# Compression sums of a two-layer kernel: from VectorE products to TensorE matmuls over rows fetched back from DRAM, with the statistics of chunks 8 to 15 held in place

## The chip, the cores and the metric

The kernel runs on one core of one Trainium2 chip, as one program. The metric is device time of that core in microseconds (us). The core has TensorE (PE in the profile, its weight loads PEld), VectorE (DVE), ScalarE (ACT), GpSimd (POOL) and SyncE (SP, which here only issues DMAs). All data is float32; a float32 matmul shows as two MATMUL records in the trace.

## What is computed

A batch of 4 sequences of 512 tokens with 512 features goes through two transformer layers. Layer 0 is a compressed sparse attention with 16 heads of 128 plus a local window, and a mixture of 8 experts; layer 1 is a plain attention with 16 heads of 32 and another mixture. The part that the change touches is the start of layer 0. Cut to what matters:

```python
xn = layernorm(x)                                   # 4 x 512 x 512
w_log = (xn @ Wcmp + bcmp).reshape(4, 128, 4)       # one logit a token, groups of 4 tokens
w_cmp = softmax(w_log, axis=-1)
entries = einsum('bcr,bcrh->bch', w_cmp, xn.reshape(4, 128, 4, 512))
ck = rope(rmsnorm(entries @ Wk + bk), block_ends)   # 128 compressed keys a sequence
cv = entries @ Wv + bv                              # and their values
# every head's queries score ck, keep the 8 best and mix cv; a local window attention is added
```

So each sequence's 512 normalized rows are reduced to 128 entries, each a weighted sum of four neighbouring rows.

## The kernel before

**Chunks and copies of the input.** The 2048 tokens are 16 chunks of 128 rows; chunks 0 to 3 are sequence 0, 4 to 7 sequence 1, and so on. `acc` holds the rows in SBUF. `layernorm(n, ...)` takes the statistics of chunk n on VectorE (`bn_stats` L221, its aggregate L223, an addition L224), the inverse root on GpSimd (L225, for chunks from 4 on also L227), makes the normalized rows `xn` (on VectorE for chunks 0 to 3, on ScalarE at L234 for the others), writes them to the DRAM tensor `xnd` (L237; chunks 4 to 7 from ScalarE's queue, the others from SyncE's) and turns them on TensorE (`trx`, L242) into `xnT`, the transposed copy that every product reads (copy at L243). Before the change `xnd` is read only much later, by the expert gathers.

**Steps.** The main loop runs over 32 steps (g, b): 8 groups of two heads, and in each the 4 sequences. Step i computes the attention of its group and sequence and projects the queries, keys and values of step i+1 in between, by seven half-size products (`first`, `second`, ..., `fifth`, all matmuls at L661, VectorE sums at L696 to L725). `project(0)` stands ahead of the loop. Inside a step the order is `scores` of head 0, `first`, `scores` of head 1, `second`, `context` of head 0, `third`, `context` of head 1, `fourth`, `fifth`, `output`.

**Work hung into the first steps.** `jobs0` hangs further work into places (i, t) of the steps: sequence 0 and 1 are normalized ahead of the loop, sequence 2's chunks 8 to 11 in step 0, sequence 3's chunks 12 to 15 in step 1. `compress(b, pool)` is a generator of four parts; those of sequence 0 run ahead of the loop, and those of b = 1, 2, 3 in steps 0, 1, 2. Part 1 transposes the compression logits (`wt`, L584), makes the softmax weights `w1` and builds `wd`, 128x512, by four VectorE multiplications of the identity (L596). Part 2 spreads `wd` over all partitions by a matmul with a matrix of ones (`wB`, L599) and, for each of four feature blocks, multiplies `xnT` by it (`prod`, L603) and adds groups of four (L604) into `entT`. Part 3 multiplies `entT` by Wk and Wv (`kv`, L609) and normalizes and rotates `ck`. Part 4 turns `ck` (`trck`, L619) into `ckT`, which the scores `sp` (L744) of the sequence's step read.

**What sets the order.** The tile framework's scheduler reorders the instructions of each engine by its own estimate of when their inputs are ready; every engine then runs its list strictly in order and waits by semaphores. `tc.keep_in_program_order(x)` pins x behind the instruction that was written just before it on the same engine. In `layernorm` only the statistics of chunks below 4 are pinned (`pin`). PSUM tiles come from three rings: `mm` (3 banks: products, output), `sc` (3: scores, contexts, `wB`, `kv`) and `tr` (2: transposes). SyncE's DMA list is in order too.

Of the kernel before, what the change touches and what calls it, by code (L numbers as in the profile page):

```python
# [12 lines left out]
F32 = mybir.dt.float32  # L13
I32 = mybir.dt.int32
AF = mybir.ActivationFunctionType
ALU = mybir.AluOpType
AX = mybir.AxisListType
# [3 lines left out]
P = 128  # L21
B, S, HID = 4, 512, 512
T = B * S
NT = T // P
TC = S // P
KC = HID // P
NH, D = 16, 128
RATIO = 4
C = S // RATIO
# [20 lines left out]
def two_layers(ctx: ExitStack, tc: tile.TileContext, a: dict, out: bass.AP, large: bass.AP):  # L50


    FEW = 32
    nc = tc.nc
    V, G, A, PE = nc.vector, nc.gpsimd, nc.scalar, nc.tensor
# [14 lines left out]
    sp0 = setup.enter_context(tc.tile_pool(name="setup", bufs=2, side="right"))  # L70


    def psum(tag, name):
        return ps.tile([P, 512], F32, tag=tag, name=name, bufs={"mm": 3, "sc": 3, "tr": 2}[tag])
# [53 lines left out]
    xnT = keep.tile([P, KC, T], F32, tag="xnT", name="xnT")  # L128
    x_v = a["x"].rearrange("(n p) h -> p n h", p=P)

    xnd = dram.tile([T, HID], F32, tag="xnd", name="xnd")
# [43 lines left out]

    ident = const.tile([P, P], F32, tag="ident", name="ident")
    make_identity(nc, ident)
    nhalf = const.tile([P, 8], F32, tag="nhalf", name="nhalf")
    G.memset(nhalf, -0.5)
    A.activation(small.tile([P, 8], F32, tag="warm", name="warm", bufs=1), nhalf, AF.Exp)  # L180
    ones_sq = const.tile([P, P], F32, tag="ones_sq", name="ones_sq")
    G.memset(ones_sq, 1.0)
# [32 lines left out]
    def layernorm(n, pool, bank, scaled=False):  # L215

        pin = tc.keep_in_program_order if n < TC else (lambda x: x)
        st = small.tile([P, 6], F32, tag="st", name=f"st_{n}")  # L220
        pin(V.bn_stats(st, acc[:, n, :]))  # L221
        mv = small.tile([P, 2], F32, tag="mv", name=f"mv_{n}")
        V.bn_aggr(mv, st)  # L223
        V.tensor_scalar(mv[:, 1:2], mv[:, 1:2], 1e-5, None, ALU.add)  # L224
        G.tensor_tensor(mv[:, 1:2], mv[:, 1:2], nhalf[:, 0:1], ALU.pow)  # L225
        if scaled:
            G.tensor_scalar(mv[:, 0:1], mv[:, 0:1], mv[:, 1:2], -1.0, ALU.mult, ALU.mult)  # L227
        made = {}

        def rows():  # L230
            tag = "ctx" if n in (2, 3) else "xn"
            xn = made["xn"] = (wk0 if n in (2, 3) else pool).tile([P, HID], F32, tag=tag, name=f"xn_{n}")
            if scaled:
                A.activation(xn, acc[:, n, :], AF.Identity, scale=mv[:, 1:2], bias=mv[:, 0:1])  # L234
            else:
                pin(V.tensor_scalar(xn, acc[:, n, :], mv[:, 0:1], mv[:, 1:2], ALU.subtract, ALU.mult))
            (nc.scalar if TC <= n < 2 * TC else nc.sync).dma_start(out=xnd[ts(n, P), :], in_=xn)  # L237

        def turn():
            xn, tr = made["xn"], bank("tr", f"trx_{n}")  # L240
            for k in range(KC):
                pin(PE.transpose(tr[:, ts(k, P)], xn[:, ts(k, P)], ident))  # L242
            A.copy(xnT[:, :, ts(n, P)], tr.rearrange("p (k t) -> p k t", k=KC))  # L243
        return rows, turn
# [302 lines left out]
    lv = const0.tile([P, TC, 3, D + 1], F32, tag="lv", name="lv")  # L547
# [11 lines left out]
    def squares(x, n, pool, name, extra=1.0):  # L559

        sq = pool.tile([P, D], F32, tag="sq", name=f"sq_{name}", bufs=1)
        ss = small.tile([P, n], F32, tag=f"ss{n}", name=f"ss_{name}", bufs=4)
        for h in range(n):
            A.activation(sq, x[:, h, :], AF.Square, accum_out=ss[:, h : h + 1])  # L564
        G.tensor_scalar(ss, ss, D * 1e-6, extra, ALU.add, ALU.mult)
        G.tensor_tensor(ss, ss, nhalf[:, 0:n], ALU.pow)  # L566
        return ss

    def rotate(x, tt1, tt2, n, pool, name):

        r1 = pool.tile([P, n, R], F32, tag="r1", name=f"r1_{name}", padded_shape=[P, 6, R] if n > 1 else None, bufs=1)
        r2 = pool.tile([P, n, R], F32, tag="r2", name=f"r2_{name}", padded_shape=[P, 6, R] if n > 1 else None, bufs=1)
        V.tensor_tensor(r1, x[:, :, 0:R], tt1, ALU.mult)
        V.tensor_tensor(r2[:, :, 0:32], x[:, :, 32:R], tt2[:, :, 0:32], ALU.mult)
        V.tensor_tensor(r2[:, :, 32:R], x[:, :, 0:32], tt2[:, :, 32:R], ALU.mult)
        V.tensor_tensor(x[:, :, 0:R], r1, r2, ALU.add)

    def compress(b, pool):

        w_row = row_w[b]  # L580

        wt = psum("tr", f"wt_{b}")
        for r in range(RATIO):
            PE.transpose(wt[:, ts(r, P)], w_row.rearrange("p (c r) -> p r c", r=RATIO)[:, r, :], ident)  # L584
        w1 = pool.tile([P, RATIO], F32, tag="w1", name=f"w1_{b}", bufs=1)
        V.tensor_reduce(w1, wt.rearrange("p (r k m) -> p r k m", k=KC, m=FEW)[:, :, :, 0], AX.X, ALU.add)
        V.tensor_scalar(w1, w1, bcmp[:, 0:1], None, ALU.add)
        mx = pool.tile([P, 1], F32, tag="wmx", name=f"wmx_{b}", bufs=1)
        V.tensor_reduce(mx, w1, AX.X, ALU.max, negate=True)
        sm = pool.tile([P, 1], F32, tag="wsm", name=f"wsm_{b}", bufs=1)  # L590
        A.activation(w1, w1, AF.Exp, bias=mx, accum_out=sm)
        V.reciprocal(sm, sm)
        V.tensor_scalar(w1, w1, sm, None, ALU.mult)
        wd = pool.tile([P, C, RATIO], F32, tag="prod", name=f"wd_{b}", bufs=1)
        for r in range(RATIO):
            V.tensor_scalar(wd[:, :, r], ident, w1[:, r : r + 1], None, ALU.mult)  # L596
        yield
        wB = psum("sc", f"wB_{b}")
        PE.matmul(wB, lhsT=ones_sq, rhs=wd.rearrange("p c r -> p (c r)"), start=True, stop=True)  # L599
        entT = pool.tile([P, KC, C], F32, tag="entT", name=f"entT_{b}", bufs=1)  # L600
        for k in range(KC):
            prod = pool.tile([P, C, RATIO], F32, tag="prod", name=f"prod_{b}_{k}", bufs=1)
            V.tensor_tensor(prod.rearrange("p c r -> p (c r)"), xnT[:, k, ts(b, S)], wB, ALU.mult)  # L603
            V.tensor_reduce(entT[:, k, :], prod, AX.X, ALU.add)  # L604
        yield
        kv = psum("sc", f"kv_{b}")
        for i, w in enumerate((wk, wv)):
            for k in range(KC):
                PE.matmul(kv[:, ts(i, D)], lhsT=entT[:, k, :], rhs=w[:, k, :],  # L609
                          start=(k == 0), stop=(k == KC - 1))  # L610
        V.tensor_tensor(cv[:, b, 0:D], kv[:, ts(1, D)], bkv[:, 1, :], ALU.add)
        ck = pool.tile([P, 1, D], F32, tag="ck", name=f"ck_{b}", bufs=1)
        V.tensor_tensor(ck[:, 0, :], kv[:, ts(0, D)], bkv[:, 0, :], ALU.add)
        ss = squares(ck, 1, pool, f"ck_{b}")
        rotate(ck, t1c, t2c, 1, pool, f"ck_{b}")
        A.activation(ck[:, 0, :], ck[:, 0, :], AF.Copy, scale=ss[:, 0:1])
        yield
        tr = psum("tr", f"trck_{b}")
        PE.transpose(tr[:, 0:C], ck[:, 0, :], ident)  # L619
        A.activation(ckT[:, b, :], tr[:, 0:C], AF.Copy, scale=turned[:, 0:1])  # L620
        yield
# [16 lines left out]
    def project(i):  # L638
# [3 lines left out]
        g, b = steps[i]  # L642
# [15 lines left out]
        def product(nm, x, w, c):  # L658
            p = psum("mm", f"{nm}_{i}_{c}")[:, 0 : 3 * D]
            for k in range(2):  # L660
                PE.matmul(p, lhsT=x[:, k, ts(c, P)], rhs=w[:, k, :], start=(k == 0), stop=(k == 1))  # L661
            return p
# [49 lines left out]
        by_head = lambda x: x.rearrange("p c (h d) -> p c h d", d=D)  # L712
# [8 lines left out]
        def fifth():  # L721
            u2 = u["u2"]
            for c in range(2):
                p3 = product("p3", xs3, w_b[:, 2:4, :], c).rearrange("p (h d) -> p h d", d=D)
                V.tensor_tensor(lv[:, c, :, 0:D], p3, by_head(u2)[:, c], ALU.add)  # L725
            x = lv[:, :, 2, 0:D]
            ss = squares(x, TC, wk0, f"{i}_k", float(D))
            rotate(x, t1[:, :, 2, :], t2[:, :, 2, :], TC, wk0, f"{i}_k")
            for h in range(HG):
                norm_k[(i, h)] = [ss[:, t : t + 1] if h else sq[t // 2][:, ds(t % 2 * 3 + 2, 1)] for t in range(TC)]  # L730

        xs0, xs1, xs2, xs3 = (xs[n] for n in range(4))
        return qkT, sums_x, first, second, third, fourth, fifth, turn_queries, turn_keys

    def scores(i, h, qkT):
# [135 lines left out]
    def start_sequence(n):  # L871
        for f in layernorm(n, sp0, psum, n >= TC):
            f()
# [4 lines left out]
    for b in range(1, B):  # L878
        i = b - 2
# [77 lines left out]
    for n in range(3 * TC):  # L957
        i, t = 29 + n // TC, n % TC
# [480 lines left out]
    for g in range(NG):  # L1439
        b, j = groups1[g]  # L1440
# [743 lines left out]
```

## Time and profile before

| | |
|---|---|
| median of 3 runs | 2075.16 us (2073.69 to 2077.63) |
| the profiled execution | 2074.66 us, span of its core 2072.6 us |
| PE busy | 2017.7 us, 97% |
| DVE busy | 1452.0 us, 70% |
| ACT busy | 867.9 us, 42% |
| POOL busy | 754.3 us, 36% |
| granted TensorE clock, mean | 0.995 |
| region of the change | about 30 to 195 us of the span: the first projection and steps 0 to 2 |

The busy share of PE counts matmul records whose ends are modelled, so a group of n records that follow each other is best measured from its start to the next group's start. A row of the timeline gives start, busy time, engine, line, operation, tiles and shapes, the number of instructions merged into it, and in brackets the idle time before it with what ended it.

### The profile page before, as it was taken

Reading aid. Unit: us, or ns where it says so; the run is one execution under the profiler, and the core shown is the slowest. Engines: PE = TensorE matmul, PEld = TensorE weight load, DVE = VectorE, ACT = ScalarE, POOL = GpSimd, SP = SyncE. Lnnn points to the kernel's source line nnn. Section 1 sums busy time; section 2 is a strip of 40 time slices with the busy share of each in tenths; the row PEclk is TensorE's granted clock in tenths of the full one; section 3 lists DMA queues with packets and bytes.
Section 4 is the critical chain, followed back from the end, with each engine's and each line's share of the span. In section 5 each row is a group of like instructions: output and inputs, shape, how many; then the busy total and the mean of one; then the engine's idle time right before and its main releaser. Section 6 shows DMA issues by size and latency. Waiting matters only on the chain.

```text
span 2072.6 us, 27984 instructions
## 1 busy us (share of the span) xinstructions
PE 2017.7 (97%) x9130; PEld 1205.3 (58%) x9130; DVE 1452.0 (70%) x3543; ACT 867.9 (42%) x2600; POOL 754.3 (36%) x761
## 2 busy tenths in 40 slices
PE   6999999999999999999999999999999999999997
PEld 4666666666666666666666666666334445445442
DVE  7888967666766666676667778787596555557775
ACT  4554444444444443444444455454243432333332
POOL 4422244443423333344333444353114332332550
PEclk9999999999999999999999999999999999999999
DMA  7102133333333343234443222121317765773551
GB/s 250 68 31 62 42 118 120 143 108 103 130 130 104 109 155 103 92 135 166 183 170 116 70 76 85 42 72 62 119 51 244 263 243 196 257 243 123 158 163 52
DMA packets 98906, 267.23 MB, mean 129 GB/s; under 512 B 14400, under 2 KB 27840, under 8 KB 87488
## 3 DMA queue, kind: packets, MB, share of 16 engines
q0 software_dynamic: 27072, 148.91, 21.4%
q1 hardware_dynamic: 70528, 114.34, 16.4%
q10 hardware_dynamic: 1152, 2.10, 0.3%
q8 instruction: 75, 1.23, 0.2%
q14 instruction: 79, 0.65, 0.1%
HBM read 222.05 MB, written 42.73 MB: 128 GB/s over the span
## 4 chain that ended last, share of the span: by engine, by line
PE 81%; DVE 8%; ACT 3%; POOL 2%; DMA 2%; issue 1%; SPq 0%; ACTq 0%; POOLq 0%; DVEq 0%
PE p L661 23%; PE hp_r L518 12%; PE op L828 10%; PE st L753 4%; PE st L1224 3%; PE qp L1200 3%; PE sp L744 3%; PE cx L1238 2%; PE ca L797 2%; PE o L1307 2%; PE trm_r L506 2%; PE vp L1160 1%; PE trq L681 1%; PE trk L687 1%; PE cc L800 1%
## 5 line engine op out<-in xcount | busy, mean ns | idle before, releaser
L828 PE MATMUL op<-Wo,cT 128*128 128x512 f32 x512 | 230.6, 598 | 5.3 <-DVE lv L725 2.9
L518 PE MATMUL hp_r<-we_r,xT_r 128*128 128x512 f32 (+1 forms) x592 | 224.8, 596 | 0.0
L470 POOL DMA_INDIRECT xr_r<-xnd,rows_r x72 | 89.4, 1242 | 331.6 <-PE trm_r L506 298.2
L761 POOL TENSOR_TENSOR lT<-lT,lmask 128x512 f32<-128x512 f32 (+1 forms) x128 | 157.6, 1244 | 140.8 <-ACT lT L757 140.6
L661 PE MATMUL p<-wT,x 128*128 128x384 f32 x512 | 179.6, 493 | 0.5 <-DVE wT L119 0.5
L661 PE MATMUL p<-wB,x 128*128 128x384 f32 x512 | 175.9, 488 | 4.0 <-DVE u L717 4.0
L661 PE MATMUL p<-wA,xnT 128*128 128x384 f32 x512 | 174.0, 492 | 0.2 <-DVE u L696 0.2
L828 PEld LDWEIGHTS op<-Wo,cT 128*128 128x128 f32 x512 | 92.0, 190 | 115.0 <-issue 77.2
L564 ACT ACTIVATE sq<-qb 128x128 f32<-128x128 f32 x384 | 118.9, 310 | 93.0 <-DVE qb L710 44.9
L1226 ACT ACTIVATE pT<-st 128x1024 f32<-128x1024 f32 x128 | 123.7, 1014 | 62.7 <-PE st L1224 57.0
L518 PEld LDWEIGHTS hp_r<-we_r,xT_r 128*128 128x128 f32 (+1 forms) x592 | 83.8, 170 | 97.3 <-issue 91.8
L831 DVE TENSOR_TENSOR acc<-acc,op 128x512 f32<-128x512 f32 x128 | 87.4, 685 | 69.4 <-PE op L828 69.0
L661 PEld LDWEIGHTS p<-wB,x 128*128 128x128 f32 x512 | 93.9, 190 | 68.5 <-issue 10.2
L661 PEld LDWEIGHTS p<-wT,x 128*128 128x128 f32 x512 | 94.5, 193 | 63.5 <-issue 6.7
L661 PEld LDWEIGHTS p<-wA,xnT 128*128 128x128 f32 x512 | 95.6, 193 | 61.0 <-issue 2.9
L675 ACT ACTIVATE qb<-qb,ss 128x128 f32<-128x128 f32 x256 | 81.9, 390 | 110.7 <-POOL ss L566 108.6
L508 ACT COPY xT_r<-trm_r 128x512 f32<-128x512 f32 x72 | 41.8, 581 | 198.0 <-PE hp_r L518 188.3
L757 ACT ACTIVATE lT<-st,ss 128x256 f32<-128x256 f32 (+1 forms) x128 | 47.2, 449 | 175.4 <-PE st L753 175.3
L753 PE MATMUL st<-qkT 128*128 128x256 f32 (+1 forms) x512 | 110.4, 357 | 0.0
L534 POOL DMA_INDIRECT row_r<-yd,slot_r x64 | 74.2, 1160 | 94.0 <-DVE row_r L1341 35.8
L753 PEld LDWEIGHTS st<-qkT 128*128 128x128 f32 x512 | 93.1, 193 | 11.4 <-issue 1.4
L566 POOL TENSOR_TENSOR ss<-ss,nhalf 128x6 f32<-128x6 f32 x64 | 95.7, 1496 | 5.3
(360 smaller groups left out, 4334.2 us busy)
## 6 DMA issues: line engine op xcount, KB each, us to landing
x<-xsd SPq DMA_DIRECT2D x112, 256.0 KB, 3.1
yd<-yr_r SPq DMA_DIRECT2D x72, 256.0 KB, 3.4
wA<-in_wA SPq DMA_DIRECT2D x16, 384.0 KB, 3.6
wB<-in_wB SPq DMA_DIRECT2D x16, 384.0 KB, 7.6
xnd<-xn SPq DMA_DIRECT2D x24, 256.0 KB, 2.0
accd<-acc SPq DMA_DIRECT2D x18, 256.0 KB, 2.0
acc<-in_x SPq DMA_DIRECT2D x16, 256.0 KB, 4.9
Wo<-in_Wo SPq DMA_DIRECT2D x8, 512.0 KB, 3.6
```

What stands on the lines that cost most here:

```text
L470: G.indirect_dma_start(out=out, out_offset=None, in_=src, in_offset=at_rows(idx))
L518: PE.matmul(hp[ts(h, m), :], lhsT=xT[:, k, ts(h, m)], rhs=w[:, ts(k, HID)], start=(k == 0), stop=(k == KC - 1))
L534: G.indirect_dma_start(out=x, out_offset=None, in_=self.yd, in_offset=at_rows(self.r.slot[:, k, n : n + 1]))
L564: A.activation(sq, x[:, h, :], AF.Square, accum_out=ss[:, h : h + 1])
L566: G.tensor_tensor(ss, ss, nhalf[:, 0:n], ALU.pow)
L661: PE.matmul(p, lhsT=x[:, k, ts(c, P)], rhs=w[:, k, :], start=(k == 0), stop=(k == 1))
L675: A.activation(x[:, j, :], x[:, j, :], AF.Copy, scale=sq[t][:, j : j + 1])
L753: PE.matmul(st[:, ds((t % 2) * 256, n)], lhsT=qkT[:, HG + h, ts(t, P)], rhs=qkT[:, h, ds(t * P, n)], start=True, stop=True)
L761: G.tensor_tensor(dst, dst, lmask.rearrange("p a w j -> p (a w j)")[:, 0:n], ALU.mult)
L828: PE.matmul(op, lhsT=cT[:, h, ts(t, P)], rhs=wo[:, h, :], start=(h == 0), stop=(h == HG - 1))
L831: V.tensor_tensor(acc[:, n, :], acc[:, n, :], op, ALU.add)
L1226: A.activation(pt[:, ts(pair, 2), :], st, AF.Exp, scale=SCALE1)
```

## The change

The weighted sums move to TensorE. `compress` first fetches the sequence's 512 normalized rows back from `xnd`, 1 MB, into `rows_` (one buffer for all four sequences, from SyncE's queue). `wd` shrinks from 128x512 to 128x128: a 128x32 matrix `fold`, made once on GpSimd, takes the place of the identity. TensorE turns `wd` (`trw`), ScalarE copies it (`wsel`), four matmuls of 32 columns each, one for each chunk, sum the rows into one PSUM bank (`ep`), ScalarE copies that (`ent`), TensorE turns it (`tre`, four transposes) and ScalarE copies it into `entT`. The matmul `wB` and the VectorE products and sums are gone.

Two pins are added: `bn_stats` of chunks 8 to 15 of layer 0 is kept in program order on VectorE, and so is the last addition of `fifth` in `project(0)`, the projection ahead of the loop.

```diff
+    fold = sp0.tile([P, FEW], F32, tag="fold", name="fold", bufs=1)
     nhalf = const.tile([P, 8], F32, tag="nhalf", name="nhalf")
     G.memset(nhalf, -0.5)
+    G.tensor_tensor(fold, ident[:, ts(0, FEW)], ident[:, ts(1, FEW)], ALU.add)
+    for n in (2, 3):
+        G.tensor_tensor(fold, fold, ident[:, ts(n, FEW)], ALU.add)
...
-        pin = tc.keep_in_program_order if n < TC else (lambda x: x)
+        pin = tc.keep_in_program_order if n < TC or scaled and n >= 2 * TC else (lambda x: x)
...
     def compress(b, pool):
         w_row = row_w[b]
+        rows_ = pool.tile([P, TC, HID], F32, tag="rows4", name=f"rows4_{b}", bufs=1)
+        nc.sync.dma_start(out=rows_, in_=xnd[ts(b, S), :].rearrange("(n p) h -> p n h", p=P))
...
-        wd = pool.tile([P, C, RATIO], F32, tag="prod", name=f"wd_{b}", bufs=1)
+        wd = pool.tile([P, FEW, RATIO], F32, tag="wd", name=f"wd_{b}", bufs=1)
         for r in range(RATIO):
-            V.tensor_scalar(wd[:, :, r], ident, w1[:, r : r + 1], None, ALU.mult)
+            V.tensor_scalar(wd[:, :, r], fold, w1[:, r : r + 1], None, ALU.mult)
         yield
-        wB = psum("sc", f"wB_{b}")
-        PE.matmul(wB, lhsT=ones_sq, rhs=wd.rearrange("p c r -> p (c r)"), start=True, stop=True)
+        tr = psum("tr", f"trw_{b}")
+        PE.transpose(tr[:, 0:P], wd.rearrange("p c r -> p (c r)"), ident)
+        wsel = pool.tile([P, P], F32, tag="wd", name=f"wsel_{b}", bufs=1)
+        A.copy(wsel, tr[:, 0:P])
+        ep = psum("sc", f"ent_{b}")
+        for n in range(TC):
+            PE.matmul(ep[ts(n, FEW), :], lhsT=wsel[:, ts(n, FEW)], rhs=rows_[:, n, :], start=True, stop=True)
+        ent = pool.tile([P, HID], F32, tag="lr", name=f"ent_{b}", bufs=1)
+        A.copy(ent, ep)
+        tr = psum("tr", f"tre_{b}")
+        for k in range(KC):
+            PE.transpose(tr[:, ts(k, C)], ent[:, ts(k, P)], ident)
         entT = pool.tile([P, KC, C], F32, tag="entT", name=f"entT_{b}", bufs=1)
-        for k in range(KC):
-            prod = pool.tile([P, C, RATIO], F32, tag="prod", name=f"prod_{b}_{k}", bufs=1)
-            V.tensor_tensor(prod.rearrange("p c r -> p (c r)"), xnT[:, k, ts(b, S)], wB, ALU.mult)
-            V.tensor_reduce(entT[:, k, :], prod, AX.X, ALU.add)
+        A.copy(entT, tr.rearrange("p (k c) -> p k c", k=KC))
...
-                V.tensor_tensor(lv[:, c, :, 0:D], p3, by_head(u2)[:, c], ALU.add)
+                last_ = V.tensor_tensor(lv[:, c, :, 0:D], p3, by_head(u2)[:, c], ALU.add)
+            if i == 0:
+                tc.keep_in_program_order(last_)
```

In the built program the lists of the five engines are the same as before from step 3 on, but for the line numbers and a few neighbouring DMAs on SyncE's list; between the first projection and the end of step 2 they are reordered.

## The prediction

> **What bounds the kernel.** I read the page first, then the list of what TensorE (PE) waited for between 30 and 205 us, then the granted clock by windows, then the timeline of each engine there. Chip times, durations and pitches (start to next start) are rows of the one profiled execution.
>
> ```profile
> PE 2017.7 (97%) x9130; PEld 1205.3 (58%) x9130; DVE 1452.0 (70%) x3543; ACT 867.9 (42%) x2600; POOL 754.3 (36%) x761
> ```
>
> PE is the bound. A VectorE (DVE) saving is worth only what PE waited for it. In the region of the change that is little:
>
> ```profile
> PE wB L599 <- DVE wd L596: 2.3, 2, 1.2
> PE trck L619 <- ACT ck L616: 1.5, 1, 1.5
> ```
>
> The columns are total us, times, longest. The two waits for `wd` stand at 116.98 (1.01) and 165.35 (1.25), the one for `ck` at 59.17 (1.48). Only the last is followed by a slower clock (third column from the right):
>
> ```profile
> 62.00:64.00 2.00, 2.00 (x9) 1.73 (x9) 1.54 (x11) 0.21 (x1) 1.92 (x3) 0.59 0.35 131
> 64.00:66.00 2.00, 2.00 (x9) 1.73 (x9) 2.00 (x10) 1.56 (x5) 1.63 (x2) 0.55 0.08 32
> ```
> ```profile
> 62.48 3.20 PE L753 MATMUL st<-qkT 128*128 128x256 f32 x8
> 68.53 1.68 PE L753 MATMUL st<-qkT 128*128 128x256 f32 x8
> ```
>
> The same eight records took 1.5 us more there. So all that PE loses here is 1.48 + 1.5 + 1.01 + 1.25 = 5.2 us: the ceiling of any gain.
>
> **The sums themselves, on PE.** The nearest rows:
>
> ```profile
> 43.62 1.02 PE L599 MATMUL wB<-wd,ones_sq 128*128 128x512 f32 x2
> 101.90 1.06 PE L252 MATMUL lg_r<-xnT,wr 128*32 128x512 f32 x8
> 85.25 0.60 PE L820 MATMUL trc<-ident,ctx 128*128 128x128 f32 x4
> ```
>
> `wB` goes: 0.86 (43.62 to 44.48). The four 32-column matmuls have the form of the logits `lg_r`: 0.99 for all four (101.90 to 102.89). Five transposes at 0.11 (four take 0.44) add 0.55. That is +0.68 a sequence, 2.7 for four, all on the bound.
>
> **On DVE** each sequence loses four products and four sums at a pitch of 0.59, 4.7, and `wd` falls from 0.92 to 0.4 to 0.92 (ends: the pitch of a 128x4 scaling, and the old row); I take 0.6. This 5 us of relief was on PE's path only in the waits above.
>
> ```profile
> 73.43 0.67 DVE L603 TENSOR_TENSOR prod<-xnT,wB 128x512 f32<-128x512 f32 x1
> 74.69 0.66 DVE L604 TENSOR_REDUCE entT<-prod 128x128 f32<-128x512 f32 x1
> 70.29 0.92 DVE L596 TENSOR_SCALAR wd<-ident,w 128x128 f32<-128x128 f32 x4
> ```
>
> **On ScalarE (ACT)** three copies, 0.3 + 0.5 + 0.5 by pitch, 1.4 a sequence, on an engine about half idle here. The path they lie on is PE, copy, PE, copy, PE. Behind `trw` PE has one half product (0.65) before the four matmuls, against copy and hand-offs of 0.5 to 0.7; behind those three context matmuls (0.66) before `tre`, against 0.7 to 0.8. So 0.1 to 0.2 each when ACT is free.
>
> **`fold`**: three small GpSimd (POOL) operations at about 2 us; POOL is idle from 2.1 to 4.69 there, so nothing (0.6 if that gap were not there).
>
> **The rows' DMA.** No row shows a 1 MB fetch. Bounds: 3.6 us (`Wo`, 512 KB) and 7.6 (`wB` weights, two of 384 KB in a busy stretch); with 295 GB/s at 44 to 48 us I take 6. Sequence 0's is issued at about 41, behind the four `xsd` stores, lands by 47.5 and is read at 49.6: hidden, each us over 8.5 costs one. The group 1 weights and `b2` rows behind it land some 4 us later, about 52.5; POOL's L120 waits for them, and the roots for `ck` (about 57) stand behind it: 3 us of cover. The fetches of sequences 1 to 3 wait on SyncE for chunk rows written to DRAM and for the one buffer, and the `cv0s` copy, the `xsd` stores and the group 1 `wA` load stand behind them; by the row writes they go out at about 51, 97 and 141 and are read at 75, 118 and 165. Hidden.
>
> **Sequence 0's turn.** Before, `kv` ends at 57.89, with its first matmuls spread between the `entT` pieces. The new PE list from 43.62: `trw` 0.11, 12 half products 7.74, sums 0.99, `tre` 0.44, `trq` 0.44, `trx` 0.44, then `kv` 1.76; I let it end at 55.6. But then logits need chunk 7's copy, which ACT has behind the copies of `entT`, `trq`, chunk 6 and `trk` and the square of `ck`: 57.7, a wait of 1.2. And `ck`, 2.75 behind `kv` before, has that `trk` copy (0.65) ahead of its square: `trck` at 59.0, another 0.35. Scores `sp` start at 60.2 for 61.44, with `trg` (0.44) still to do: gain 0.9. The waits together are as long as before, so I leave the half clock in.
>
> **The pins: the dear part.** Before, chunk 8's rows were made at 48.80, 19 us ahead of their transposes; nothing waited. Now its statistics stand behind `wd` of sequence 1, and the chain runs through four engines, while PE's list is in order: everything queued behind the transposes waits. Rows:
>
> ```profile
> 71.54 0.68 DVE L221 BATCH_NORM_STATS2 st<-acc 128x6 f32<-128x512 f32 x1
> 78.00 0.54 POOL L225 TENSOR_TENSOR mv<-mv,nhalf 128x1 f32<-128x1 f32 x1 [3.23 <-DVE mv L223]
> 78.64 0.27 POOL L227 TENSOR_SCALAR mv<-mv 128x1 f32<-128x1 f32 x1
> 83.64 0.83 ACT L234 ACTIVATE xn<-acc,mv 128x512 f32<-128x512 f32 x1
> ```
>
> Chunk 8, counted from the start of `sp` of step 0. DVE: before, `wd` began 8.85 later (61.44 to 70.29); the new list drops 1.1 of statistics from that stretch and puts a subtraction (0.60) and a rotation (0.47) in, so again 8.85. Then `wd` 0.6, statistics 0.6, a match 0.28, aggregate 0.1, a product sum 0.47, L224 0.1; POOL 1.0; ACT 0.8; hand-offs 0.1: 12.8. PE: `sp` 1.04, `trg` 0.44, `st` 1.5 (3.0 at half clock), `trk` 0.5, `wt` 0.48, `sp` 0.9, `st` 1.5, six half products at 0.645, 3.87: 10.2 to 11.7. It waits 1.1 to 2.6: 2.0.
>
> Chunk 12, counted from `wt` in step 1 (111.45 before). The new list puts `wd` behind the top-8 of head 1, two product sums, the mask steps (held up while POOL masks, as 1.04 for L769 at 118.96 shows) and the softmax weights: 7.8. Two statistics 9.0; aggregates and the sum of the sixth product 9.65; POOL 10.65; ACT 11.5. PE: 0.47 + 0.9 + 1.5 + 11 half products 7.1 = 10.0, plus 0.3 since that sum frees a PSUM bank late. Wait 1.2 + 0.3 = 1.5.
>
> Smaller waits, laid out the same way: chunk 9's `tre` 0.1, chunk 10 0.35, chunk 11 1.15 (statistics behind a context sum), chunk 14 0.65, `wsel` of step 1 behind two row scalings on ACT 0.9, its `tre` 0.2: 3.35. One wait gives the next slack, so I count half: 1.7. In step 2 no chunk is left; `wd` is about as late as before, PE has 1.9 more work ahead of it, and waits 0.8 for 1.25.
>
> **The clock.** A wait of 1.48 us was followed by half clock, those of 1.01 and 1.25 were not; chunk 8's 2.0 lies above. I add the 1.5 of the row. [...]
>
> **The sum.** Sequence 0: -0.9. Step 0: +0.7 + 2.0. Step 1: +0.7 - 1.0 + 1.5. Step 2: +0.7 - 1.25 + 0.8. Small waits +1.7, clock +1.5. Total +6.4, rounded. From step 3 on the order is the same and PE the bound, so it is carried to the end: 2074.66 + 6.4 = 2081.1; the profiled run lies 0.5 below the median of 2075.16, so 2081.5 in these terms; I say 2081.
>
> **Rivals.**
> *A, not slower: the pinned rows arrive in time.* VectorE is lighter by 5 us a sequence; if the chain of chunk 8 takes under 10.2 us from `sp`, the transposes never wait, and the old waits go: -5.2 + 2.7 = -2.5, 2072.7. For it: DVE is busy 19.1 of 20 us at 60 to 80. Against: the work ahead of `wd` in its list is not less. It decides below a chain of 10.2 to 11.7.
> *B, the clock multiplies the waits.* All small waits in full (+1.65) and a half clock behind chunk 11, chunk 12 and `wsel` too (+3 to +4.5): 2085.7 to 2087.2. For it: three waits of about 1.2. Against: 1.25 brought none before.
> *C, the rows come late.* 1 MB at the pace of the page's mean 129 GB/s is 8 us, and two stragglers would cost 2 to 3: 2083.5.
> That the sums stay on DVE is excluded: its built list has no product or sum of L603 and L604.
>
> **Chances and range.** Forecast 0.5 (2077.5 to 2085), A 0.25 (2070 to 2076), B 0.15, C 0.05, others 0.05. A measurement of this kernel tells about 0.2% (4.15 us) from no change. The forecast is beyond it with 0.39 and within with 0.11; A within with 0.19, faster with 0.06; B 0.15 and C 0.04 slower; the others 0.01, 0.03, 0.02. Faster 0.07, same 0.33, slower 0.60. Range: from A's 2072.7 less 1 to B's 2087.2, 2071.5 to 2087.5. The forecast's own is 2077.5 to 2085.
>
> **What would show it.** Right: in the waits, `trx` on ACT's `xn` in steps 0 and 1, 3 to 6 us in total, the longest about 2 near 72 to 74; a half clock behind it; `sp` of step 0 at about 60.2, of step 1 2 to 4 us later than 102.89, and step 3's 5 to 7 later than 193.31; `wd` no longer waited for in step 1; the sums near 0.99 for eight records; the DMA wait of `ep` nil. Wrong: `trx` never waits and step 3 starts early (A), or `ep` waits for its rows (C), or the difference arises behind step 3.

## The result, and the profile after

The changed kernel takes 2088.46 us (median of 4 runs, 2087.69 to 2089.31) against 2075.61 for the kernel before beside it: +12.85 us, ratio 1.0062, 95% interval 1.0044 to 1.0079. The profiled execution took 2089.19 us, its span is 2087.3.

The page's row of TensorE shows almost the busy time of before (2018.5 us for 2017.7), with 44 more instructions; the DVE row fell by 15.0 us. The span grew by 14.7, so most of that is time in which PE stood idle:

```profile
PE 2018.5 (97%) x9174; PEld 1203.0 (58%) x9174; DVE 1437.0 (69%) x3511; ACT 873.7 (42%) x2612; POOL 757.4 (36%) x764
```

What PE waited for between 30 and 205 us (total us, times, longest). The waits for `wd` and `ck` of before are down to 0.8 and nil; six waits for normalized rows took their place:

```profile
PE trx L248 <- ACT xn L240: 10.5, 6, 5.9
PE lg_r L258 <- ACT xnT L249: 1.1, 1, 1.1
PE trw L608 <- DVE wd L605: 0.8, 1, 0.8
```

The granted clock by windows (third column from the right). The half clock moved from 62 to 66 us to 74 to 81 us and doubled in length:

```profile
72.00:74.00 2.00, 0.00 (x0) 1.00 0.00 0
74.00:76.00 2.00, 0.46 (x2) 0.51 0.00 0
76.00:78.00 2.00, 2.00 (x9) 0.50 0.35 131
78.00:80.00 2.00, 2.00 (x4) 0.50 0.00 0
80.00:82.00 2.00, 2.00 (x14) 0.79 0.36 135
```

PE's timeline: the sums (eight records, no DMA wait in front), the first scores, the `st` records that took 3.20 us before and are at full clock now, and chunk 8's transposes:

```profile
48.83 1.06 PE L614 MATMUL ent<-rows,wsel 128*32 128x512 f32 x8
59.33 1.16 PE L763 MATMUL sp<-ckT,qkT 128*128 128x32 f32 x8
60.76 1.68 PE L772 MATMUL st<-qkT 128*128 128x256 f32 x8
65.61 4.04 PE L678 MATMUL p<-wT,x 128*128 128x384 f32 x12
75.54 1.12 PE L248 MATMUL trx<-ident,xn 128*128 128x128 f32 x4 [5.90 <-ACT xn L240]
```

Executions differ in when the first transpose or first spread of the softmax weights (`trw` or `wB` of sequence 0) begins: between 42.55 and 44.87 us in the traces of this study. So the runs are compared by stretches: from that instruction (A) to the first `sp` of step 0, and from each step's first `sp` to the next. All in us:

| kernel | A to step 0 | step 0 | step 1 | step 2 | sum, less before |
|---|---|---|---|---|---|
| before | 17.82 | 41.45 | 46.23 | 44.19 | 0 |
| changed | 16.51 | 52.30 | 49.67 | 44.51 | +13.3 |
| `sums_only` | 17.54 | 44.74 | 46.95 | 44.51 | +4.1 |
| `pin_only` | 18.66 | 49.57 | 51.09 | 43.65 | +13.3 |
| `pin_8_11` | 16.52 | 52.70 | 46.96 | 44.50 | +11.0 |
| `pin_12_15` | 17.50 | 46.39 | 49.69 | 44.53 | +8.4 |
| `stats_first` | 16.51 | 46.70 | 50.82 | 44.52 | +8.9 |
| `late_turn` | 16.52 | 49.44 | 49.67 | 44.51 | +10.5 |
| `wd_act` | 16.51 | 50.36 | 50.02 | 44.63 | +11.8 |
| `masks_dve` | 16.51 | 46.52 | 49.68 | 44.52 | +7.5 |

The changed kernel's 13.3 agrees with the medians' 12.85: step 0 +10.85, step 1 +3.44, step 2 +0.32, ahead of step 0 -1.31. From the first `sp` of step 3 to the end, where the lists are the same, single executions take between 1878.4 us (`pin_only`) and 1882.6 (`pin_12_15`), 1881.5 in the changed kernel and 1879.3 before. So single spans can't rank kernels that differ by a few us: the stretches show the mechanism, the ratios the time.

### The profile page after: what moved, and what is told of

Its sections match the earlier page's. It is cut to its first block, busy times and chain, and to the rows that moved or that the text cites. A ratio compares the mean times of both kernels' runs of the same rounds, so it can differ in the third digit from the quotient of the medians.

```text
span 2087.3 us, 28068 instructions
## 1 busy us (share of the span) xinstructions
PE 2018.5 (97%) x9174; PEld 1203.0 (58%) x9174; DVE 1437.0 (69%) x3511; ACT 873.7 (42%) x2612; POOL 757.4 (36%) x764
## 4 chain that ended last, share of the span: by engine, by line
PE 75%; DVE 9%; ACT 3%; POOL 2%; DMA 2%; issue 2%; ACTq 0%; DVEq 0%; POOLq 0%
PE p L678 22%; PE hp_r L524 12%; PE op L847 10%; PE st L772 4%; PE st L1243 3%; PE qp L1219 2%; PE sp L763 2%; PE cx L1257 2%; PE ca L816 2%; PE trm_r L512 2%; PE o L1326 1%; DVE pS L1263 1%; PE vp L1179 1%; PE trq L698 1%; PE cb L819 1%
## 5 line engine op out<-in xcount | busy, mean ns | idle before, releaser
L571 POOL TENSOR_SCALAR ss<-ss 128x6 f32<-128x6 f32 x64 | 33.0, 516 | 180.4 <-ACT sq L570 180.2
```

## The experiments

**What the two halves cost alone.** `sums_only` takes both pins from the changed kernel:

```diff
-        pin = tc.keep_in_program_order if n < TC or scaled and n >= 2 * TC else (lambda x: x)
+        pin = tc.keep_in_program_order if n < TC else (lambda x: x)
...
             if i == 0:
-                tc.keep_in_program_order(last_)
+                pass
```

> The changed kernel without the pin on the statistics of chunks 8 to 15 (the pin on the last sum of the first projection moves nothing in the built lists, and goes too); the sums stay on TensorE. Theory L (late rows: the pin costs, the sums do not): the waits of TensorE's transposes on xn, 10.5 us in the changed kernel, fall below 1 us, the half clock near 72 to 84 us goes (about 3 us), and the time is 2074 to 2078 us, sequence 0's 2 us gain kept. Theory S (the chain of transposes and copies that the sums go through costs): xn is no longer waited for, but the time stays above 2082 us, with new waits for wsel, entT or wd. Theory R (the fetched rows are late): a wait for a DMA stands before the four 32-column matmuls.

`pin_only` makes the reverse edit of the `pin` line in the kernel before.

> The kernel before with the pin on the statistics of chunks 8 to 15 as its only edit; the sums stay on VectorE. Theory L: xn is waited for by 8 us or more in steps 0 and 1 and the time is 2083 to 2090 us. Theory S: the pin is cheap when VectorE's order is otherwise the old one, below 2079 us.

`sums_only`: 2079.83 us, ratio 1.0028 (1.0016 to 1.0041). `pin_only`: 2086.32, ratio 1.0063 (1.0049 to 1.0077). So both theories were half right: the pin alone makes the whole loss, and the sums alone cost too. `sums_only` lies above the 2074 to 2078 of theory L and below the 2082 of theory S; `pin_only` has the time of L, but waits for `xn` by 3.2 us and not by 8. In the code `pin` covers, beside the statistics, the four transposes of each of these chunks on TensorE; in the built programs this and the pin of `last_` move nothing, and the statistics' pin on VectorE does it all. PE's waits of `sums_only`, then of `pin_only`:

```profile
PE trw L608 <- DVE wd L605: 2.5, 2, 1.7
PE p L678 <- DVE u L734: 1.3, 2, 1.1
PE trs L798 <- ACT s L789: 0.9, 1, 0.9
```
```profile
PE wB L599 <- DVE wd L596: 4.6, 3, 2.3
PE trx L242 <- ACT xn L234: 3.2, 5, 0.9
PE trk L687 <- ACT xnT L243: 2.3, 2, 1.8
```

With the sums alone `xn` is never waited for; the rest is PE's added work and later `wd`, `u` and `s` in step 0. With the pin alone the late VectorE list shows at other readers, `wd` above all. The two costs (+4.1 and +13.3) don't add: under the pin the sums make step 0 2.7 us longer and step 2 0.9, but step 1 1.4 and the stretch ahead of step 0 2.15 shorter, nothing in total. No run takes that apart.

**Which chunks.** The condition of `pin` cut to chunks 8 to 11, and to 12 to 15:

```diff
-        pin = tc.keep_in_program_order if n < TC or scaled and n >= 2 * TC else (lambda x: x)
+        pin = tc.keep_in_program_order if n < TC or scaled and 2 * TC <= n < 3 * TC else (lambda x: x)
```

> The changed kernel with the statistics pinned for chunks 8 to 11 only (those made in step 0). By the starts of the scores of steps 1 to 3 in the runs so far, the pin costs step 0 some 7.5 us more than the sums alone, the stretch ahead of step 0 some 3 us less, and step 1 some 2.7 us more. If these parts add, this kernel has step 0 of the changed kernel (start of sp of step 1 at about 111.5 us) and step 1 of the sums alone (47 us long): 2084 to 2087 us, 2.7 us below the changed kernel. Rival: step 1's loss is a consequence of step 0's late rows, and stays: within 1.5 us of 2088.5.

> The changed kernel with the statistics pinned for chunks 12 to 15 only (those made in step 1). If the parts add: steps 0 as with the sums alone (sp of step 1 at about 107 us), step 1 about 49.7 us long for 47, xn waited for by 2 to 3 us in step 1 only, 2081 to 2084 us. Rival (step 1's loss comes from step 0): 2079 to 2080.5 us, as the sums alone.

2086.28 us (ratio 1.0059, 1.0047 to 1.0072) and 2083.80 (1.0046, 1.0033 to 1.0059). Step 1 is independent: 46.96 without its own pin, though step 0 was as late as in the changed kernel, and 49.69 with it. Step 0's loss belongs to chunks 8 to 11. Not foreseen: the pin of chunks 12 to 15 alone already makes step 0 1.65 us longer than the sums alone, since `trw` then stands earlier on PE's list:

```profile
72.16 0.45 PE L608 MATMUL trw<-ident,wd 128*128 128x128 f32 x1 [3.59 <-DVE wd L605]
```

**Where the pinned rows stand.** `stats_first` writes chunk 8's and 12's statistics ahead of the compression part of the same step; `late_turn` leaves them, but writes chunk 8's transposes two places later:

```diff
+    for n in range(2 * TC, NT): jobs0.append(((n // TC - 2, n % TC), lambda n=n: start_sequence(n)))
...
-        for t in range(TC):
-            if b > 1:
-                jobs0.append(((i, t), lambda n=b * TC + t: start_sequence(n)))
```
```diff
-        for f in layernorm(n, sp0, psum, n >= TC):
-            f()
-
+        if n != 8: [f() for f in layernorm(n, sp0, psum, n >= TC)]
+        else: r8, turn8[8] = layernorm(n, sp0, psum, True); r8()
+    turn8 = {}; jobs0.append(((0, 2), lambda: turn8[8]()))
```

> The changed kernel with the pinned statistics of chunks 8 and 12 written ahead of the compression part of the same step, so that they are not behind wd on VectorE's list. Theory L with the chain behind wd as the culprit: chunk 8's statistics run about 5 us earlier, the wait of 5.9 us and the half clock behind it go, chunk 12's 1 us goes, and the time is 2077 to 2081 us. If the pin costs wherever it stands (rows cannot be ready because VectorE has no room in steps 0 and 1), waits of the same total come at other chunks, and the time stays at 2086 to 2090 us.

> The changed kernel with all pins, but chunk 8's transposes written two places later in the program (after the third projection part), so that they no longer stand ahead of the sums on TensorE's list. Theory P (TensorE's list put the transposes too early; what is behind them could have run): the 5.9 us wait and the 2.7 us of half clock go, no other wait above 1.5 us comes, 2079 to 2082 us. Theory V (VectorE's list is late as a whole in step 0, so the next reader of its results waits in the transposes' place): trw waits 3 to 5 us for wd, half clock follows, 2085 to 2089 us.

`stats_first`: 2086.36 us, 1.0061 (1.0047 to 1.0075). The long wait and the half clock go and step 0 is 5.6 us shorter than in the changed kernel, but step 1 is 1.2 longer: waits of 5.4 us for `xn` stay, spread over six chunks, and one of 2.1 ahead of a product. By the table it gains 4.4 us and stands at 1.0043; the interval of its ratio begins just above that. The 2077 to 2081 of theory L are missed; the time is the rival's (2086 to 2090), though the waits for `xn` are half of the changed kernel's 10.5 and not the same total. `late_turn`: 2087.16, 1.0063 (1.0050 to 1.0076). Theory V holds in kind: other readers of VectorE's results wait in the transposes' place, though twice 2.2 us and without half clock:

```profile
69.42 0.55 PE L798 MATMUL trs<-ident,s 128*128 128x128 f32 x3 [2.17 <-ACT s L789]
73.44 0.30 PE L608 MATMUL trw<-ident,wd 128*128 128x128 f32 x1 [2.18 <-DVE wd L605]
```

So it is not one instruction that is misplaced: moved on PE's list or on VectorE's, the waits come up elsewhere.

**Why VectorE is late: held beside GpSimd.** VectorE's timeline of the changed kernel, then GpSimd's, in the same stretch:

```profile
63.06 1.65 DVE L670 TENSOR_TENSOR x<-x,xnT 128x512 f32<-128x512 f32 x1
64.64 1.28 DVE L787 TENSOR_TENSOR rep<-s,rep 128x320 f32<-128x320 f32 x1
65.95 1.44 DVE L788 SCALAR_TENSOR_TENSOR s<-rep,s 128x320 f32<-128x320 f32 x1
69.33 2.48 DVE L605 TENSOR_SCALAR wd<-fold,w 128x32 f32<-128x32 f32 x4
```
```profile
62.89 2.68 POOL L780 TENSOR_TENSOR lT<-lT,lmask 128x512 f32<-128x512 f32 x2
65.53 1.51 POOL L671 TENSOR_TENSOR x<-xnT,x 128x512 f32<-128x512 f32 x1
69.27 2.21 POOL L780 TENSOR_TENSOR lT<-lT,lmask 128x512 f32<-128x512 f32 x2 [2.22 <-ACT lT L776]
```

`rep`, `s` and `wd` each end about 0.35 us behind the end of a GpSimd operation (at 65.57, 67.04 and 71.48 us). "Held" stands here for the longer time beside GpSimd; by what mechanism, no run shows. `wd_act` makes `wd` on ScalarE; `masks_dve` takes step 0's four masks to VectorE itself:

```diff
-            V.tensor_scalar(wd[:, :, r], fold, w1[:, r : r + 1], None, ALU.mult)
+            A.activation(wd[:, :, r], fold, AF.Copy, scale=w1[:, r : r + 1])
```
```diff
-            G.tensor_tensor(dst, dst, lmask.rearrange("p a w j -> p (a w j)")[:, 0:n], ALU.mult)
+            (V if i == 0 else G).tensor_tensor(dst, dst, lmask.rearrange("p a w j -> p (a w j)")[:, 0:n], ALU.mult)
```

> The changed kernel with the four scalings wd made on ScalarE in place of VectorE; all pins as they are. Theory H (VectorE held while GpSimd masks was the part of the chain that was sized too small: wd took 2.48 us): chunk 8's statistics begin some 2.5 us earlier, its wait falls from 5.9 to 3.0 to 4.0 us, and the time is 2084 to 2087 us. Rival: the hold belongs to the stretch, not to the operation, so that the statistics are held in wd's place; the wait stays above 5 us and the time within 2 us of 2088.5.

> The changed kernel with step 0's four mask products (L780, 128x512 and 128x384 for each head) on VectorE in place of GpSimd; all pins as they are, and TensorE's list has chunk 8's transposes at the same place. Theory H (the chain to chunk 8's rows is long because VectorE is held while GpSimd masks): in the changed kernel x L670, rep L787, s L788 and wd L605 took 1.65, 1.28, 1.44 and 2.48 us; they fall to about 0.7, 0.5, 0.5 and 0.5, 4.7 us in all, the four masks add 2.1 us ahead of wd, and the wait of 5.9 us falls to 2.5 to 4 us; 2083 to 2086.5 us. Rival (the length of VectorE's list as such, holds or not): the wait stays above 5 us and the time within 1.5 us of 2088.5.

`wd_act`: 2086.16 us, 1.0062 (1.0048 to 1.0075); the wait is 3.52, as theory H had it, and step 0 is 1.9 us shorter, a gain too small for the ratio to show. The statistics of chunk 8 were not held in `wd`'s place: they took their 0.69 us. `masks_dve`: 2082.22 us, 1.0043 (1.0029 to 1.0056), a little better than expected. VectorE's timeline there, and PE's wait for chunk 8:

```profile
65.06 0.68 DVE L670 TENSOR_TENSOR x<-x,xnT 128x512 f32<-128x512 f32 x1
65.65 0.48 DVE L787 TENSOR_TENSOR rep<-s,rep 128x320 f32<-128x320 f32 x1
66.17 1.44 DVE L788 SCALAR_TENSOR_TENSOR s<-rep,s 128x320 f32<-128x320 f32 x1
69.61 0.69 DVE L605 TENSOR_SCALAR wd<-fold,w 128x32 f32<-128x32 f32 x4
```
```profile
73.42 0.66 PE L248 MATMUL trx<-ident,xn 128*128 128x128 f32 x4 [2.85 <-ACT xn L240]
```

Three of the four are short; the fourth still stands beside the one GpSimd operation left there (L671, 65.87 to 67.27 us). The wait fell by 3.05 us, no half clock follows, and step 0 is 5.8 us shorter, over half of its loss, although VectorE has the masks on top. Not all of that is the hold. From the start of `wd` to that of the statistics is 1.8 us less (0.59 for 2.39), which is the hold alone; but in the new order about 0.9 us of the top-8 work of head 1 (L784, L785) also stands behind `wd` and no longer ahead of it. And there may be luck in it: the wait of 2.85 us lay across a point of the 3.41 us grid that the traces show (last section), with 1.55 and 1.30 us idle on its two sides; the 3.52 of `wd_act` left 2.34 idle on one side, and half clock followed.

**The rows' fetch.** `rows_only` puts the four fetches of 1 MB into the kernel before, unread:

```diff
-        w_row = row_w[b]
+        w_row, rows_ = row_w[b], pool.tile([P, TC, HID], F32, tag="rows4", name=f"rows4_{b}", bufs=1)
+        nc.sync.dma_start(out=rows_, in_=xnd[ts(b, S), :].rearrange("(n p) h -> p n h", p=P))
```

> The kernel before with the four fetches of 1 MB into rows_ as its only edit; nothing reads them, the sums stay on VectorE. Theory: the fetches are hidden: within 2 us of the kernel before (2072 to 2077 us), and no new DMA wait between 30 and 200 us. Rival R (the fetches delay what is queued behind them on SyncE or compete with it): 2 us or more slower, with a wait on weights, on the bias rows or on xsd rows behind a fetch.

2075.33 us, ratio 1.0006 (0.9997 to 1.0014): in the time it is hidden. In the trace it is not quite: ScalarE waits for a chunk's row write, as it did not before, and PE 0.65 us for the copy behind it.

```profile
49.44 0.81 ACT L234 ACTIVATE xn<-acc,mv 128x512 f32<-128x512 f32 x1 [1.04 <-DMA xnd<-xn]
```

The stretch ahead of step 0 is 1.2 us longer than before, and step 0 0.7 shorter, since no half clock comes there. In the changed kernel ScalarE has no such wait, and its list of transfers gives 5.9 us from issue to landing for a fetch.

**In search of a better kernel**, with the edits shown above put together.

> The sums on TensorE without the pin, and step 0's four mask products on VectorE. With the sums alone trw waited 1.7 us in step 0 for wd, whose scalings and those of w were held by about 2.4 us in all. Theory H: that wait falls under 0.8 us and step 0 (sp of step 0 to sp of step 1, 44.7 us with the sums alone) to 43 to 44 us; 2077 to 2079.5 us. Rival: the two masks of head 0 now ahead in VectorE's list cost what the holds gave, step 0 stays at 44.5 to 46 us, 2080 us or more.

> The sums on TensorE without the pin, wd's four scalings on ScalarE. Looks for the best form of the change: trw's waits of 2.5 us in total fall to about 1 us and the time is 2077.5 to 2079.5 us. To beat the kernel before it would have to gain more than 5 us on the sums alone, which no wait left in the list gives; 2080 us or more if ScalarE's scalings are as late as VectorE's.

> The kernel before (sums on VectorE, no added pin) with the mask products of steps 1 and 2 on VectorE. A try at a kernel that beats both. Theory H: VectorE is held less while wd is made, the waits of wB for wd in steps 1 and 2 (1.0 and 1.25 us) shrink below 1 us together, and steps 1 and 2 (46.2 and 44.2 us from sp to sp) get 1 to 2 us shorter in all: 2071.5 to 2073.5 us, at the edge of what can be told from the kernel before. Rival: the masks' own 2.1 us a step on VectorE take the place of the holds, within 1 us of the kernel before or slower.

`sums_masks` (no pin, step 0's masks on VectorE): 2079.06 us, 1.0024 (1.0014 to 1.0033), step 0 43.1. `sums_wd_act` (no pin, `wd` on ScalarE): 2077.65, 1.0016 (1.0008 to 1.0025), step 0 43.9, though `trw`'s waits did not shrink (2.7 us for 2.5): the best with sums on TensorE, still behind the kernel before. `before_masks` (masks of steps 1 and 2 on VectorE): 2074.17 against 2075.63, 0.9993 (0.9984 to 1.0002), steps 1 and 2 46.4 and 44.2: cannot be told from the kernel before, though the waits for `wd` fell from 2.3 to 0.9 us. In `sums_masks` the fetch of sequence 0 was read 0.6 us before it had landed, the only wait of PE for a fetch:

```profile
51.16 1.06 PE L614 MATMUL ent<-rows,wsel 128*32 128x512 f32 x8 [0.61 <-DMA rows<-xnd]
```

## Why the prediction fell short, step by step

The direction and the mechanism (late pinned rows stop PE, the clock falls behind the stop) were right; the size was +13.3 for +6.4, and 2088.46 lies above the range. The step that failed is the chain of chunk 8: it was priced at 12.8 us and took 16.2, so that the wait was 5.9 us for 2.0. By stretches, the prediction's terms put together:

| stretch | predicted | measured |
|---|---|---|
| ahead of step 0 | -0.9 | -1.31 |
| step 0 (0.7 + 2.0 + 1.5 + half of 1.6) | +5.0 | +10.85 |
| step 1 (0.7 - 1.0 + 1.5 + half of 1.75) | +2.1 | +3.44 |
| step 2 | +0.25 | +0.32 |

PE's busy time and its idle time in each step, from windows cut at the `sp` starts, take the sums apart (us; busy includes the time at half clock):

| kernel | step 0 busy, idle | step 1 | step 2 |
|---|---|---|---|
| before | 41.43, 0.02 | 45.20, 1.02 | 42.92, 1.27 |
| `sums_only` | 40.98, 3.76 | 46.47, 0.48 | 43.66, 0.85 |
| changed | 43.77, 8.53 | 47.14, 2.53 | 43.66, 0.85 |
| `masks_dve` | 41.04, 5.48 | - | 43.67, 0.85 |

*The copies, `fold`, the rows' DMA, step 2*: right. `fold` shows in no wait, the fetch took 5.9 us for 6, and `wd` of step 2 is waited for 0.81 for 0.8. Two slips are without weight: the three copies add up to 1.3 and not 1.4 us, and "No row shows a 1 MB fetch" holds for the region only, for the list of all transfers has five of 1 MB, at 5.4 to 10.1 us (`pw`, `woT`).

*The sums' work on PE*: too small. The records are as priced (eight at a pitch of 1.00 for 0.99), but busy time rose by 0.74 in step 2, 1.27 (`sums_only`) to 1.94 (changed) in step 1 and some 1.05 in step 0 (40.98 less 41.43, and 1.5 of half clock in the latter), for 0.68 each. Part of that is not the sums' but the order's: `pin_only`, which has none of their records, is busy 47.78 us in step 1 for 45.20. Products whose run was broken up by other work took longer here: in step 1 the sixteen records of `op` took 6.87 us in one piece before and with `sums_only`, and 7.37 in three pieces, waits left out, in the changed kernel. The prediction had no term for this.

*Sequence 0*: 0.4 us better. `lg_r` waited 1.1 for 1.2, but `trck` not at all (0.35 forecast). "I leave the half clock in" was wrong: the `st` records run at full clock, worth 1.5 us in step 0.

*The chain of chunk 8* is the step that failed (its terms add up to 12.9, not 12.8). PE came to the transposes 10.3 us behind `sp`, the low end of 10.2 to 11.7, since the half clock was gone. The chain took 16.2 us (59.33 to 75.54) for 12.8. `wd` began 10.0 us after `sp` for 8.85 and lasted 2.4 for 0.6, and from the statistics to `xn` it took 3.0 for 2.5. I had carried the old distance of `wd` over to a new order, and taken `wd` from rows beside an idle GpSimd, though I had priced GpSimd's hold for chunk 12, and though the kernel before has the four scalings beside a mask (L761, 116.44 to 117.70) in step 1:

```profile
115.81 2.03 DVE L596 TENSOR_SCALAR wd<-ident,w 128x128 f32<-128x128 f32 x4
```

So the wait was 5.9 for 2.0; in `masks_dve`, without most of the holds, the chain is 13.2 and the wait 2.85. The rows of `x`, `rep` and `s` above, each with two inputs in SBUF, took 1.65, 1.28 and 1.44 us beside GpSimd, and in `masks_dve` 0.68, 0.48 and 0.48 without it (`rep` and `s` of head 1, at 72.58 and 73.45 us); `wd`, with one such input and a column of scalars, took 2.48 for 0.69. Not everything is held: in `sums_only`, while GpSimd masked from 66.65 to 69.13 us, a match (L785) took its 0.28 us and statistics (L227) their 0.68.

*The clock*: 1.5 us forecast, 2.7 measured: from 75.54 to 80.85 us PE ran at a granted clock of 0.50, 5.3 us that by the `st` records (3.20 us at half clock, 1.68 at full in the kernel before) would have taken about half as long. That half clock came at all was right by luck: it was forecast because a wait of 2.0 is longer than one of 1.48, but waits of 2.17 and 2.18 (`late_turn`) and 2.85 (`masks_dve`) brought none.

*The small waits in step 0*: chunk 10 0.91 and chunk 11 1.71 for 0.35 and 1.15, and both counted in full; "one wait gives the next slack" did not hold. In `masks_dve` chunk 8 waits 3.05 us less, and chunks 10 and 11 wait as long, 0.92 and 1.71. In the changed kernel the statistics of chunk 10 (91.73 us) stand on VectorE's list behind a sum of the context `cc` of head 1 (91.13), and those of chunk 11 (95.42) behind the context that follows from it (95.15). TensorE made `cc` at 90.48, behind the long wait, so that wait delayed the later chains too.

Put together, step 0 is 41.45 - 1.5 (half clock gone) + 1.1 (work) + 5.9 + 0.91 + 1.71 (waits) + 2.7 (clock) = 52.3, as measured. Step 1 is 46.23 - 1.0 (`wd`) + 1.9 (work) + 2.45 (waits) = 49.6 for 49.67; its waits are chunk 12's 0.99, with 0.46 of a product ahead of it (1.2 and 0.3 forecast), and 0.35 and 0.65 for chunks 14 and 15 (0.65 and none), so there the work, with the broken runs, is the term that failed; `wsel` and `tre` (0.9 and 0.2) never waited.

Rival A fell: the chain took 16.2 us and not less than 10.2. Rival C fell: no wait for a fetch stands ahead of the sums in the changed kernel, and `rows_only` costs no time that can be told. Rival B's time (2085.7 to 2087.2) was nearest, but not by its mechanism: no later wait brought half clock; one long wait did, for twice as long. Of the signs named beforehand, the forecast that `trx` waits 3 to 6 us in total failed (10.5), `sp` of step 1 was 8.7 us later than 102.89, not 2 to 4, and that of step 3 12.5 later than 193.31, not 5 to 7.

## What to carry to other kernels

Pinning an operation on one engine moved later hand-offs of that engine too (PE waited 4.6 us for `wd` in `pin_only`, 2.3 before); price it as a chain from a fixed event to the reader, with each link's duration taken from rows with the same neighbours on the other engines. VectorE work of 0.5 to 0.7 us took 1.3 to 2.5 while GpSimd worked beside it, so when work is moved, look at what GpSimd will be doing at the new time. A saving on an engine that isn't the bound is worth the waits that it removes and the half clock behind them, here 5.2 us at most, and was outweighed here by one new stop of the engine that is: 5.9 us, and 2.7 of half clock behind it.

## What the runs showed of the hardware

**The granted clock changed on a grid of 3.41 us in these traces.** Read in windows of 0.1 us, a mixed one split by its mean, the granted clock changed at 24.83, 35.07, 62.38 and 65.79 us in the kernel before and at 22.82, 33.06, 74.02 and 80.85 in the changed one: distances of 10.24, 27.31 and 3.41, and of 10.24, 40.96 and 6.83, which are 3, 8, 1, 3, 12 and 2 times 3.41. In `wd_act`, `pin_8_11`, `pin_12_15` and `pin_only` they run from 3.41 to 40.96, all such multiples too. The half clock lasted 6.8 us behind waits of 5.9 (changed, `pin_8_11`) and 3.5 (`wd_act`), 3.4 behind 2.3 (`pin_only`) and 3.6 (`pin_12_15`). Cut at these points, into intervals of 3.41 us, the traces show from 40 us on how long PE was idle in the interval that half clock followed: 3.41 us (changed, `pin_8_11`), 3.15 (`pin_12_15`), 2.34 (`wd_act`), 2.28 (`pin_only`), but only 1.50 in the kernel before, where the rest was transposes and narrow score matmuls. Full clock followed intervals with 1.86 us idle (`stats_first`), 1.76 (`pin_only`), 1.72 and 1.57 (`late_turn`, whose two waits of 2.2 were each cut by such a point) and 1.55 and 1.30 (`masks_dve`). The wait of 1.48 of the kernel before comes in `rows_only` too, in an interval that began with half products, and full clock followed:

```profile
60.99 0.33 PE L619 MATMUL trck<-ident,ck 128*128 128x128 f32 x1 [1.48 <-ACT ck L616]
62.77 1.68 PE L753 MATMUL st<-qkT 128*128 128x256 f32 x8
```

Full clock also followed the 1.71 at 99.15 us of the changed kernel. So in these traces the length of a wait alone did not tell whether half clock followed. That its place on the grid and what shares its interval count too is my reading; which activity counts how much stays open.
